# A graph layer on one core: one-hots made slot by slot for both graphs, instead of block by block with a tensor of slot numbers

## The chip, the core and the metric

The kernel runs on one core of a Trainium2 chip. The metric is the device time of the whole program in microseconds (us): 804.08 us, the median of three runs (802.24 to 804.27). The profile is of one execution of 803.91 us, in which the span of the program's instructions is 801.1 us, with a mean granted TensorE clock of 0.995.

Engines are written as in the profile: PE is TensorE's matmuls, PEld its weight loads, DVE is VectorE, ACT ScalarE, POOL GpSimd, SP SyncE, which issues the DMAs. L747 is line 747 of the kernel before.

## The reference

There are 128 graphs of 128 nodes with 64 features each, x [128, 128, 64], and an adjacency matrix for each, adj [128, 128, 128], about 6% of it nonzero, symmetric in its pattern, with the diagonal set. Two layers follow one another, each with a residual and a normalization without gain:

```
mask = adj > 0
h[j,k,:] = relu(x[k] @ W1b-part + x[j] @ W1a/b-part + b1)      # 192 wide, for each pair (j, k)
hm[j] = sum over k of mask[j,k] * h[j,k,:]
x = layernorm(x + hm @ W2 + deg[j] * b2)                        # layer 0
a = adj @ x
o = elu(elu(a @ V1 + c1) @ V2 + c2) @ V3 + c3
x = layernorm(x + o)                                            # layer 1
```

In full, `h[j,k] = relu(x[j] @ W1a + (x[j] - x[k]) @ W1b + b1)`: a part that depends on j alone, called aj, and one that depends on k alone, called cp. The hard part is hm: a sum of relus over the neighbours k of every node j.

## The kernel before, in words

**Only neighbours are visited.** The program takes two graphs (a pair) at a time, 64 pairs in all; the hidden width of 192 is cut into three parts (c) of 64, and the two graphs (s) stand in the two halves of the 128 partitions. For each pair the nodes are sorted by falling degree. `BLOCKS` cuts the 128 sorted positions into nine blocks (p0, p1, s): positions p0 to p1 get s slots each, enough for their neighbours. A block is a unit of work. For a unit with n = s x (p1 - p0) columns:

- ACT fills an `e` bank in PSUM with aj, spread over the slots (L735).
- PE adds, by matmul with a one-hot, the column cp of the neighbour that stands in each slot (`gather`, L742 to L751): three parts k of a bf16 splitting of cp, three parts c, two graphs s, 18 matmuls of n columns. Weights of 64 columns leave half of the array's columns to each graph, so the two streams s = 0 and 1 run side by side.
- DVE takes the absolute sum over the slots (`reduce`, L756). With the sum of absolutes and a correction by degree the relus are had.

There are four `e` banks, `edges`, and unit u uses bank u mod 4; so a unit's fill waits for the reduce of the unit four before. The columns of the nine units are 162, 66, 168, 112, 168, 154, 169, 154 and 170, in this order, 1323 (E) in all.

**The one-hots.** `sort_mask` (L530) sorts the mask, takes prefix sums over the neighbours, and so has in `vp` (128 x 2 x 128, bf16) for each neighbour k (partition), graph and sorted position j the number 2 x slot + 1 if k is j's neighbour in that slot, and an even number if it isn't. A one-hot for slot t is `vp == 2t + 1`. Before, `oh` is [P, 2, E], for each block the slots one after another; nine tensor_tensors (L560) compare vp, spread over the block's slots, with `slotc`, a constant tensor of slot numbers made in the set-up (L159 to L174). Each of them has its own event, and the gather of unit i waits for that of block i. A gather reads `oh[:, s, base:base + n]`, one run without gaps.

**The order of the work.** The program has no loop at run time over the pairs; every instruction is written out, and the order on each engine is set beforehand by a planner, the class `Flow`. Work is cut into threads (Python generators: `prepare`, `sort_x`, `project_a`, `sort_mask`, `turn`, `project_c`, `unit`, `finish`) whose steps name an engine, an estimated cost, what they wait for and how many PSUM banks they want. The planner keeps a clock for each engine and takes next the step that can start first; among steps that can start about as soon on that engine, the one with the earliest due time. A thread's due time advances by `STEP` with each of its steps. `due(p, step)` is `ROUND * (p - AHEAD) + STEP * step`: preparation of pair p is due AHEAD rounds before the pair's gathers. `TURN`, `CS` and `SORT` are the steps at which `turn`, `project_c` and the sort are due. The name PORT beside an engine makes a step of DVE or GpSimd exclude the other's steps of that kind.

PE steps carry a mode: "PE:t" for matmuls with weights of 64 columns (the gathers, L480 and L694), "PE" for the others. A change of mode costs `SWITCH` = 0.1 in the plan, and a step of the other mode ranks as if it were due `HOLD` later. Weights with 64 rows (L593 in `project_c`) are a third shape on the chip, which the planner doesn't tell apart; in the profile the three shapes read 128\*64, 128\*128 and 64\*128.

`finish` (L660) does the rest of layer 0 and layer 1 for a pair. After the last pair, `dense` looks whether any node had more neighbours than its slots and would do such pairs in another way.

Of the kernel before, what the change touches and what calls it, by code (L numbers as in the profile page):

```python
# [31 lines left out]
F32 = mybir.dt.float32  # L32
BF16 = mybir.dt.bfloat16
I32 = mybir.dt.int32
AF = mybir.ActivationFunctionType
OP = mybir.AluOpType
# [6 lines left out]
BLOCKS = ((65, 83, 9), (0, 3, 22), (83, 104, 8), (3, 10, 16), (104, 128, 7), (10, 21, 14),  # L43
          (21, 34, 13), (34, 48, 11), (48, 65, 10))


@with_exitstack
def gnn_kernel(ctx: ExitStack, tc: tile.TileContext, x, adj, w1, b1, w2, b2,
               v1, c1, v2, c2, v3, c3, out):
    nc = tc.nc  # L50
# [4 lines left out]
    P = 128  # L55
# [4 lines left out]
    LAY, E = [], 0  # L60
    for p0, p1, s in BLOCKS:
        n = s * (p1 - p0)
        assert 3 * n <= 512
        LAY.append((E, n, p0, p1, s))
        E += n
    NB = len(LAY)

    cpool = ctx.enter_context(tc.tile_pool(name="consts", bufs=1))
    ctx.enter_context(tc.manual_schedule())
# [4 lines left out]
    def const(shape, dt, name, src=None, pool=cpool):  # L74
        t = pool.tile(shape, dt, name=name)
        if src is not None:
            nc.sync.dma_start(t, src)
        return t

    def temp(shape, dt, name, src=None):  # L80
        return const(shape, dt, name, src, tpool)
# [49 lines left out]
    for s in range(2):  # L131
# [7 lines left out]
                   allow_small_or_imprecise_dtypes=True)  # L139
# [4 lines left out]
                   allow_small_or_imprecise_dtypes=True)  # L144
# [10 lines left out]
                   allow_small_or_imprecise_dtypes=True)  # L155
    nc.vector.tensor_scalar(jcol, jcol, 1.0 / P, None, op0=OP.mult)


    slotf = temp([P, E], F32, "slotf")  # L159
    slots = const([P, 1], F32, "slots")  # L160
    steps = temp([P, 1], F32, "steps")
    nc.vector.memset(slots, 0.0)
    prev = 0
    for base, n, p0, p1, s in LAY:
        nc.gpsimd.iota(slotf[:, base:base + n], pattern=[[2, s], [0, p1 - p0]], base=1,
                       channel_multiplier=0, allow_small_or_imprecise_dtypes=True)
    for p0, p1, s in sorted(BLOCKS, reverse=True):

        nc.vector.tensor_scalar(steps, jcol[:, 0:1], p1 / P, float(s - prev),
                                op0=OP.is_lt, op1=OP.mult)  # L170
        nc.vector.tensor_add(slots, slots, steps)
        prev = s
    slotc = const([P, E], BF16, "slotc")
    nc.vector.tensor_copy(slotc, slotf)  # L174

    srow = const([P, 3, P], F32, "srow")
# [17 lines left out]
    for s in range(2):  # L194
        k = slice(s * F, (s + 1) * F)
# [26 lines left out]
    with tc.tile_pool(name="ps_s", bufs=2, space=bass.MemoryType.PSUM) as ps_s:  # L222
        t = ps_s.tile([P, 512], F32, name="s")
# [4 lines left out]
        t = ps_s.tile([P, 512], F32, name="s")  # L228
# [4 lines left out]
        t = ps_s.tile([P, 512], F32, name="s")  # L233
# [35 lines left out]
class Flow:  # L269
# [10 lines left out]
    NEAR = 0.1  # L280
    NEAR_PE = 0.05
    SWITCH = 0.1
    HOLD = 1

    def __init__(self, banks):
        self.clock = {}
# [45 lines left out]
    def _rank(self, th):  # L332
        engine, _, mode = th[4][0].partition(":")
        return th[0] + (self.HOLD if self._switch(engine, mode) else 0.0), th[1]

# [23 lines left out]
def sparse(tc, env):  # L359

    g = type("env", (), dict(env))
    nc, P, N, F, H, O, HB, H1, NP, E = (
        g.nc, g.P, g.N, g.F, g.H, g.O, g.HB, g.H1, g.NP, g.E)
    LAY, NB = g.LAY, g.NB
    loads, prep, work, ps_m = g.loads, g.prep, g.work, g.ps_m
# [12 lines left out]
    EV = {}  # L378


    ROUND = 11.31
    AHEAD = 3
    PACE = ROUND / NB
    STEP = 1.55
    TURN = 2
    CS = 3
    SORT = 7
    FIN = 1.5

    def due(p, step):  # L390
        return ROUND * (p - AHEAD) + STEP * step

# [30 lines left out]
    def flat(t):  # L423
        return t.rearrange("p s n -> p (s n)")

    def prepare(p):
# [103 lines left out]
    def sort_mask(p, ev):  # L530

        d, a, permb = S[p], ADJ[p], S[p]["permb"]

        def sort(t):
            for s in range(2):
                nc.tensor.matmul(t[:, s * N:(s + 1) * N], d["mk"][:, s, :], permb[:, s, :],
                                 start=True, stop=True)
            for s in range(2):
                nc.tensor.matmul(t[:, (2 + s) * N:(3 + s) * N], permb[:, s, :], identb,
                                 start=True, stop=True)  # L540
        ev, t = yield ("PE", 0.22, [ev], 1, sort)
        mtp = d["mtp"] = prep.tile([P, 2, N], BF16, name="mtp", bufs=7)
        permT = d["permT"] = prep.tile([P, 2, N], F32, name="permT", bufs=7)
        evm, = yield ("ACT", act(2 * N), [ev], 0, lambda: nc.scalar.copy(flat(mtp), t[:, :2 * N]))
        happened(evm, "mtp", p)
        ev, = yield ("ACT", act(2 * N), [ev], 0, lambda: nc.scalar.copy(flat(permT), t[:, 2 * N:]))  # L546
        flow.give(t, ev)
        happened(ev, "permT", p)
        ev, vps = yield ("PE", 0.11, [evm], 1,
                         lambda vps: nc.tensor.matmul(vps[:, :2 * N], g.prefix, flat(mtp),  # L550
                                                      start=True, stop=True))
        vp = prep.tile([P, 2, N], BF16, name="vp")
        ev, = yield ("ACT", act(2 * N), [ev], 0, lambda: nc.scalar.copy(flat(vp), vps[:, :2 * N]))
        flow.give(vps, ev)
        oh = d["oh"] = prep.tile([P, 2, E], BF16, name="oh", bufs=5)
        for i, (base, n, p0, p1, sl) in enumerate(LAY):
            w = p1 - p0
            c = slice(base, base + n)
            ev, = yield ("DVE PORT", 0.08 + n / 960, [ev], 0,
                         lambda: nc.vector.tensor_tensor(  # L560
                             oh[:, :, c].rearrange("p b (s w) -> p b s w", w=w),
                             vp[:, :, p0:p1].rearrange("p b (o w) -> p b o w", o=1)
                             .to_broadcast([P, 2, sl, w]),
                             g.slotc[:, c].rearrange("p (b s w) -> p b s w", b=1, w=w)
                             .to_broadcast([P, 2, sl, w]),
                             op=OP.is_equal))
            happened(ev, "oh", p, i)

    def turn(p):

# [11 lines left out]
        happened(ev, "turned", p)  # L582
        flow.start(due(p, CS), STEP, project_c(p, ev))

# [139 lines left out]

    units = [(p, i) for p in range(NP) for i in range(NB)]

    def unit(u, ev):
        p, i = units[u]
        d = S[p]
        base, n, p0, p1, sl = LAY[i]  # L730
        w = p1 - p0
        e = edges[u % NE][:, :3 * n]
        ev, = yield ("ACT", 0.09 + 3 * n / 1200,
                     [ev, event("aj", p), [T0[0] + pace(u)] if T0 else [0.0]], 0,
                     lambda: nc.scalar.copy(  # L735
                         e.rearrange("p (c s w) -> p c s w", c=3, w=w),
                         d["aj"][:, :, p0:p1].rearrange("p c (o w) -> p c o w", o=1)
                         .to_broadcast([P, 3, sl, w])))
        if not T0:
            T0.append(ev[0])  # L740

        def gather():  # L742
            cp, oh = d["cp"], d["oh"]
            for k in range(3):
                for c in range(3):
                    for s in range(2):
                        nc.tensor.matmul(e[s * HB:(s + 1) * HB, c * n:(c + 1) * n],  # L747
                                         cp[:, k, s, c * HB:(c + 1) * HB],
                                         oh[:, s, base:base + n],
                                         start=False, stop=(k == 2), skip_group_check=True)  # L750
        ev, = yield ("PE:t", 0.03 + 0.0037 * n, [ev, event("cp", p), event("oh", p, i)], 0, gather)  # L751

        def reduce():
            if "sums" not in d:
                d["sums"] = work.tile([P, 3, N], F32, name="sums")
            nc.vector.tensor_reduce(d["sums"][:, :, p0:p1],  # L756
                                    e.rearrange("p (c s w) -> p c w s", c=3, w=w),
                                    AX.X, OP.add, apply_absolute_value=True)
        ev, = yield ("DVE", 0.07 + 3 * n / 960, [ev], 0, reduce)
        happened(ev, "sums", p, i)  # L760
        return ev

# [237 lines left out]
```

## Time and profile before

| what | busy us | share of the span of 801.1 us |
|---|---|---|
| PE | 761.2 | 95% |
| PEld | 687.5 | 86% |
| DVE | 743.1 | 93% |
| ACT | 671.3 | 84% |
| POOL | 431.2 | 54% |

| group | count | busy us | mean ns of one |
|---|---|---|---|
| PE L747, gather | 10368 | 384.5 | 228 |
| DVE L756, reduce over slots | 576 | 338.7 | 606 |
| ACT L735, fill of e | 576 | 312.0 | 553 |
| DVE L560, one-hots | 576 | 172.0 | 335 |

Busy time is the time in which at least one instruction of the group is running. Matmuls are pipelined and their ends are modelled: one of 228 ns doesn't occupy TensorE for 228 ns, and successive ones overlap. So for PE the distances between starts tell more than the durations. The same is true of DVE to a smaller degree.

The first gather starts at 41.5 us and the last at 779.6. Ahead of that are the set-up (constants, 26 us) and the first preparations, behind it the last pairs' `finish`.

### The profile page before, as it was taken

To read this page: it belongs to the slowest core of one execution; us is meant where nothing else is said; L and a number is where in the kernel's file an instruction comes from. 1 tells how busy PE (TensorE), PEld (TensorE's weight loads), DVE (VectorE), ACT (ScalarE), POOL (GpSimd) and SP (SyncE) were. 2 spreads that over 40 slices of the span, in tenths; PEclk is the share of its full clock that TensorE was granted. 3 is DMA by queue.
4 is the path that set the end of the run, shared out by engine and by line. 5 is a ranking of instruction groups with operands and counts; after the bars stand their busy time and mean duration, and the time that the engine had idled before them with its cause. 6 is when DMAs were issued, how large, how long until landed. Compare 5 with 4: busy or idle time off the path is not lost.

```text
span 801.1 us, 35941 instructions
## 1 busy us (share of the span) xinstructions
PE 761.2 (95%) x14550; PEld 687.5 (86%) x14551; DVE 743.1 (93%) x2477; ACT 671.3 (84%) x1858; POOL 431.2 (54%) x787
## 2 busy tenths in 40 slices
PE   2499999999999999999999999999999999999994
PEld 1378889998999999999999999999999999999993
DVE  6689999999999999999999999999999999999983
ACT  0387888988898889889988988898999889988963
POOL 2154465566465556555655665565556556655643
PEclk9999999999999999999999999999999999999997
DMA  1100101111101110110111011101101110111000
GB/s 35 49 3 23 26 19 26 26 22 30 25 20 29 27 28 20 29 27 19 30 30 26 19 30 29 26 20 30 27 21 28 29 26 19 30 29 26 10 10 17
DMA packets 63934, 19.91 MB, mean 25 GB/s; under 512 B 46545, under 2 KB 63762, under 8 KB 63762
## 3 DMA queue, kind: packets, MB, share of 16 engines
q1 hardware_dynamic: 63762, 17.55, 9.6%
q8 instruction: 116, 1.90, 1.0%
q14 instruction: 56, 0.46, 0.2%
HBM read 13.27 MB, written 4.19 MB: 22 GB/s over the span
## 4 chain that ended last, share of the span: by engine, by line
PE 90%; DVE 3%; DMA 2%; SPq 2%; ACT 1%; issue 1%; POOL 0%; ACTq 0%; DVEq 0%; POOLq 0%
PE e L747 43%; PE m L670 6%; PE m L494 6%; PE m L593 5%; PE m L718 4%; PE m L711 3%; PE m L704 3%; PE m L687 3%; PE m L575 2%; PE m L480 2%; PE m L694 2%; PE m L674 1%; PE m L596 1%; DMA adj<-in_adj_dram 1%; PE m L513 1%; PE m L550 1%
## 5 line engine op out<-in xcount | busy, mean ns | idle before, releaser
L747 PE MATMUL e<-oh,cp 128*64 128x162 bf16 (+3 forms) x10368 | 384.5, 228 | 1.5 <-ACT e L735 1.4
L747 PEld LDWEIGHTS <-cp 128*64 128x64 bf16 x10368 | 351.6, 110 | 19.0 <-issue 13.4
L756 DVE TENSOR_REDUCE sums<-e 128x54 f32<-128x486 f32 (+8 forms) x576 | 338.7, 606 | 10.8 <-PE e L747 2.9
L735 ACT COPY e<-aj 128x504 f32<-128x504 f32 (+6 forms) x576 | 312.0, 553 | 41.5 <-DVE sums L756 39.9
L560 DVE TENSOR_TENSOR oh<-vp,slotc 128x336 bf16<-128x336 bf16 (+6 forms) x576 | 172.0, 335 | 0.7 <-PE e L747 0.5
L632 POOL TENSOR_SCALAR ve<-st 128x2 f32<-128x2 f32 x128 | 25.1, 196 | 245.3 <-DVE st L625 238.9
L633 POOL TENSOR_TENSOR rs<-ve,mhalf 128x2 f32<-128x2 f32 x128 | 89.2, 697 | 10.7
L527 POOL TENSOR_TENSOR corr<-ea,sa 128x384 f32<-128x384 f32 x64 | 66.3, 1035 | 38.1 <-DVE ea L520 37.9
L612 POOL TENSOR_TENSOR cp<-r,cp 128x512 bf16<-128x512 f32 x64 | 74.3, 1161 | 10.5 <-ACT cp L610 10.5
L508 POOL TENSOR_TENSOR sa<-aj,srow 128x384 f32<-128x384 f32 x64 | 64.7, 1011 | 15.5 <-ACT aj L501 15.5
L665 POOL TENSOR_TENSOR hm<-sums,corr 128x384 f32<-128x384 f32 x64 | 64.4, 1006 | 9.3 <-DVE sums L756 9.3
L653 ACT ACTIVATE e<-m,mone 128x256 f32<-128x256 f32 x128 | 60.6, 474 | 9.6 <-PE m L704 5.8
L501 ACT ACTIVATE aj<-m,b1c 128x128 f32<-128x128 f32 x192 | 56.7, 368 | 4.9 <-PE m L494 1.7
L656 DVE SCALAR_TENSOR_TENSOR h<-e,m 128x256 f32<-128x256 f32 x128 | 52.9, 413 | 8.5 <-ACT e L653 8.2
L494 PE MATMUL m<-xsT,wad 128*128 128x128 f32 x384 | 59.0, 290 | 0.0
L670 PE MATMUL m<-w2d,hm 128*128 128x128 f32 x384 | 58.4, 288 | 0.7 <-POOL hm L665 0.4
L607 DVE TENSOR_TENSOR r<-m,cp 128x256 f32<-128x256 f32 x128 | 52.6, 413 | 0.1
L643 ACT ACTIVATE x<-y,nb,rs 128x64 f32<-128x64 f32 x128 | 50.7, 458 | 2.1 <-POOL nb L636 2.0
L494 PEld LDWEIGHTS m<-xsT,wad 128*128 128x128 f32 x384 | 48.9, 193 | 3.9 <-ACT permT L546 0.2
L457 DVE SCALAR_TENSOR_TENSOR cmp<-m,keyc,tie 128x128 bf16<-128x128 f32 x128 | 39.7, 347 | 13.3 <-PE m L550 11.1
L670 PEld LDWEIGHTS m<-w2d,hm 128*128 128x128 f32 x384 | 47.9, 192 | 1.8 <-POOL hm L665 0.7
L593 PE MATMUL m<-wc,turned 64*128 64x256 f32 x256 | 45.7, 432 | 0.0
(170 smaller groups left out, 1379.6 us busy)
## 6 DMA issues: line engine op xcount, KB each, us to landing
adj<-in_adj_dram SPq DMA_DIRECT2D x64, 128.0 KB, 2.3
xx<-in_x_dram SPq DMA_DIRECT2D x64, 64.0 KB, 2.2
out_dram<-o SPq DMA_DIRECT2D x64, 64.0 KB, 1.7
degs<-ys SPq DMA_DIRECT2D x64, 1.0 KB, 1.7
w1a<-in_L_gnn_W_dram SPq DMA_DIRECT2D x2, 48.0 KB, 2.1
w1b<-in_L_gnn_W_dram SPq DMA_DIRECT2D x2, 48.0 KB, 2.2
w2s<-in_L_gnn_W_dram SPq DMA_DIRECT2D x2, 48.0 KB, 2.2
b1c<-in_L_gnn_b_dram SPq DMA_DIRECT2D x6, 0.2 KB, 2.3
```

The source lines that it names most:

```text
L494: nc.tensor.matmul(aps[:, c * N:(c + 1) * N], g.wad[:, c, :], xsT, start=True, stop=True)
L508: evs, = yield ("POOL PORT", 0.95, [have], 0, lambda: nc.gpsimd.tensor_mul(sa, aj, g.srow))
L527: ev, = yield ("POOL PORT", 1.05, [ev, evs], 0, lambda: nc.gpsimd.tensor_sub(corr, ea, sa))
L560: lambda: nc.vector.tensor_tensor(oh[:, :, c].rearrange("p b (s w) -> p b s w", w=w), vp[:, :, p0:p1].rearrange("p b (o w) -> p b o w", o= ...
L593: nc.tensor.matmul(cps[s][:, :cols], d["turned"][k, 2, :], g.wc[k, :], start=True, stop=False)
L612: lambda: nc.gpsimd.tensor_sub(cp[:, 2], r1, cp[:, 1]))
L633: nc.gpsimd.tensor_tensor(rs, ve, g.mhalf, op=OP.pow)
L665: lambda: nc.gpsimd.tensor_sub(hm, d["sums"], d["corr"]))
L670: nc.tensor.matmul(yb[:, :2 * O], hm[:, c, :], flat(g.w2d[:, c]), start=(c == 0), stop=False)
L735: lambda: nc.scalar.copy(e.rearrange("p (c s w) -> p c s w", c=3, w=w), d["aj"][:, :, p0:p1].rearrange("p c (o w) -> p c o w", o=1) .to_br ...
L747: nc.tensor.matmul(e[s * HB:(s + 1) * HB, c * n:(c + 1) * n], cp[:, k, s, c * HB:(c + 1) * HB], oh[:, s, base:base + n], start=False, stop ...
L756: nc.vector.tensor_reduce(d["sums"][:, :, p0:p1], e.rearrange("p (c s w) -> p c w s", c=3, w=w), AX.X, OP.add, apply_absolute_value=True)
```

## The change

The one-hots of a pair are made slot by slot instead of block by block. For slot k, one tensor_scalar compares both graphs' `vp[:, :, :w]` with the immediate 2k + 1 and writes two rows of w elements; w is `WIDE[k]`, the last position that has more than k slots, made even. So there are 14 (`ROWS`) such instructions, with w = 128 seven times and then 104, 84, 66, 48, 34, 34, 22. The remaining eight slots, which only positions 0 to 10 have, are made by one tensor_tensor for each graph, with a `slotc` that is now only 8 x 10.

The rows lie in one tile `oh` of [P, EW], EW = 3858 elements: those of the first graph start at 134 k, those of the second at 3730 - 128 k (`RUN`), so that the long rows of the one fill the gaps behind the short rows of the other. A gather of block (p0, p1, s) now reads s rows of p1 - p0 elements at a constant distance of 134 or -128 elements. The purpose is that a comparison with an immediate reads one tensor instead of two.

A gather waits for the whole pair's one-hots (`event("oh", p)`), not its block's. `oh` has four buffers instead of five. The planner's numbers change too: HOLD, ROUND, AHEAD, STEP, TURN, CS, and the estimated cost of the one-hots.

```diff
+ROWS = 14
+RUN = ((0, 134), (3730, -128))
...
+    NS = max(s for p0, p1, s in BLOCKS)
+    WIDE = [max(p1 for p0, p1, s in BLOCKS if s > k) for k in range(NS)]
+    WIDE[ROWS:] = [WIDE[ROWS]] * (NS - ROWS)
+    WIDE = [w + w % 2 for w in WIDE]
...
-    slotf = temp([P, E], F32, "slotf")
+    slotf = temp([P, NS - ROWS, WIDE[ROWS]], F32, "slotf")
...
-    for base, n, p0, p1, s in LAY:
-        nc.gpsimd.iota(slotf[:, base:base + n], pattern=[[2, s], [0, p1 - p0]], base=1,
-                       channel_multiplier=0, allow_small_or_imprecise_dtypes=True)
+    nc.gpsimd.iota(slotf, pattern=[[2, NS - ROWS], [0, WIDE[ROWS]]], base=2 * ROWS + 1,
+                   channel_multiplier=0, allow_small_or_imprecise_dtypes=True)
...
-    HOLD = 1
+    HOLD = 5
...
-    ROUND = 11.31
-    AHEAD = 3
+    ROUND = 11.19
+    AHEAD = 4
     PACE = ROUND / NB
-    STEP = 1.55
-    TURN = 2
-    CS = 3
+    STEP = 1.47
+    TURN = 8
+    CS = 7
...
-        oh = d["oh"] = prep.tile([P, 2, E], BF16, name="oh", bufs=5)
-        for i, (base, n, p0, p1, sl) in enumerate(LAY):
-            w = p1 - p0
-            c = slice(base, base + n)
-            ev, = yield ("DVE PORT", 0.08 + n / 960, [ev], 0,
+        oh = d["oh"] = prep.tile([P, g.EW], BF16, name="oh", bufs=4)
+        WIDE = g.WIDE
+        for k in range(ROWS):
+            w = WIDE[k]
+            at = [b + k * step for b, step in RUN]
+            rows = onehots(oh, at[0], [[at[1] - at[0], 2], [1, w]])
+            last, = yield ("DVE PORT", 0.07 + 2 * w / 3840, [ev], 0,
+                         lambda: nc.vector.tensor_scalar(rows, vp[:, :, :w], 2.0 * k + 1.0, None,
+                                                         op0=OP.is_equal))
+        w, k = WIDE[ROWS], g.NS - ROWS
+        for s, (b, step) in enumerate(RUN):
+            last, = yield ("DVE PORT", 0.08 + k * w / 1920, [ev], 0,
                          lambda: nc.vector.tensor_tensor(
-                             oh[:, :, c].rearrange("p b (s w) -> p b s w", w=w),
-                             vp[:, :, p0:p1].rearrange("p b (o w) -> p b o w", o=1)
-                             .to_broadcast([P, 2, sl, w]),
-                             g.slotc[:, c].rearrange("p (b s w) -> p b s w", b=1, w=w)
-                             .to_broadcast([P, 2, sl, w]),
+                             onehots(oh, b + ROWS * step, [[step, k], [1, w]]),
+                             vp[:, s:s + 1, :w].to_broadcast([P, k, w]), g.slotc,
                              op=OP.is_equal))
-            happened(ev, "oh", p, i)
+        happened(last, "oh", p)
...
-                                         oh[:, s, base:base + n],
+                                         onehots(oh, RUN[s][0] + p0,
+                                                 [[RUN[s][1], sl], [1, w]]),
                                          start=False, stop=(k == 2), skip_group_check=True)
-        ev, = yield ("PE:t", 0.03 + 0.0037 * n, [ev, event("cp", p), event("oh", p, i)], 0, gather)
+        ev, = yield ("PE:t", 0.03 + 0.0037 * n, [ev, event("cp", p), event("oh", p)], 0, gather)
```

More of the change, by code (lines that the diff above doesn't have):

```diff
@@ L66, in gnn_kernel @@
     NB = len(LAY)
+    NS = max(s for p0, p1, s in BLOCKS)
+    WIDE = [max(p1 for p0, p1, s in BLOCKS if s > k) for k in range(NS)]
+    WIDE[ROWS:] = [WIDE[ROWS]] * (NS - ROWS)
+    WIDE = [w + w % 2 for w in WIDE]
+    used = sorted((b + k * step, b + k * step + WIDE[k]) for b, step in RUN for k in range(NS))
+    assert used[0][0] == 0 and all(a[1] <= b[0] for a, b in zip(used, used[1:]))
+    EW = used[-1][1]
     cpool = ctx.enter_context(tc.tile_pool(name="consts", bufs=1))
@@ L172, in gnn_kernel @@
         prev = s
-    slotc = const([P, E], BF16, "slotc")
+    slotc = const([P, NS - ROWS, WIDE[ROWS]], BF16, "slotc")
     nc.vector.tensor_copy(slotc, slotf)
@@ L554, in sort_mask, with onehots @@
         flow.give(vps, ev)
-        oh = d["oh"] = prep.tile([P, 2, E], BF16, name="oh", bufs=5)
-        for i, (base, n, p0, p1, sl) in enumerate(LAY):
-            w = p1 - p0
-            c = slice(base, base + n)
-            ev, = yield ("DVE PORT", 0.08 + n / 960, [ev], 0,
-                         lambda: nc.vector.tensor_tensor(
-                             oh[:, :, c].rearrange("p b (s w) -> p b s w", w=w),
-                             vp[:, :, p0:p1].rearrange("p b (o w) -> p b o w", o=1)
-                             .to_broadcast([P, 2, sl, w]),
-                             g.slotc[:, c].rearrange("p (b s w) -> p b s w", b=1, w=w)
-                             .to_broadcast([P, 2, sl, w]),
+        oh = d["oh"] = prep.tile([P, g.EW], BF16, name="oh", bufs=4)
[10 more added lines that the diff above has]
+            last, = yield ("DVE PORT", 0.08 + k * w / 1920, [ev], 0,
+                         lambda: nc.vector.tensor_tensor(
+                             onehots(oh, b + ROWS * step, [[step, k], [1, w]]),
+                             vp[:, s:s + 1, :w].to_broadcast([P, k, w]), g.slotc,
                              op=OP.is_equal))
-            happened(ev, "oh", p, i)
+        happened(last, "oh", p)
+    def onehots(oh, offset, ap):
+        t = oh[:, offset:offset + 1]
+        return bass.AP(tensor=t.tensor, offset=t.offset, ap=[t.ap[0]] + ap)
     def turn(p):
```

## The prediction

> **What bounds the kernel now.** I read the page first (busy shares, slices, chain), then two windows from the middle of the run, then the order of TensorE's instructions there, then the DVE groups by shape.
>
> From the page, the busy shares and the chain of work that ended last:
>
> ```profile
> PE 761.2 (95%) x14550; PEld 687.5 (86%) x14551; DVE 743.1 (93%) x2477; ACT 671.3 (84%) x1858; POOL 431.2 (54%) x787
> ...
> PE 90%; DVE 3%; DMA 2%; SPq 2%; ACT 1%; issue 1%; POOL 0%; ACTq 0%; DVEq 0%; POOLq 0%
> ```
>
> 90% of the chain is TensorE. Two windows of the steady part (columns: PE, PEld, DVE, ACT, POOL busy, clock, DMA share, GB/s):
>
> ```profile
> 300.00:400.00 100.00, 100.00 (x1964) 91.64 (x1962) 96.66 (x322) 90.35 (x252) 59.14 (x108) 1.00 0.11 26
> 400.00:500.00 100.00, 100.00 (x1974) 91.90 (x1973) 96.95 (x321) 90.35 (x250) 55.71 (x101) 1.00 0.11 26
> ```
>
> PE is at 100%, but DVE is close behind, so neither number says how much slack there is. The order of TensorE's work decides it (start us, us, engine, line):
>
> ```profile
> 401.50 0.61 PE L718 MATMUL m<-v3s,h 128*128 128x64 f32 x4
> 402.03 0.81 PE L747 MATMUL e<-oh,cp 128*64 128x154 bf16 x18
> 402.66 0.41 PE L694 MATMUL m<-turned,x 128*64 128x128 f32 x4
> 402.88 2.12 PE L747 MATMUL e<-oh,cp 128*64 128x169 bf16 x54
> 404.83 0.38 PE L480 MATMUL m<-permf,xx 128*64 128x128 f32 x4
> 405.05 1.09 PE L747 MATMUL e<-oh,cp 128*64 128x162 bf16 x36
> 406.07 0.23 PE L513 MATMUL m<-srow,small 128*128 128x128 bf16 x1
> ...
> 409.22 0.27 PE L550 MATMUL m<-mtp,prefix 128*128 128x256 bf16 x1
> 409.43 1.97 PE L747 MATMUL e<-oh,cp 128*64 128x168 bf16 x54
> 411.32 0.70 PE L593 MATMUL m<-wc,turned 64*128 64x256 f32 x4
> 411.96 0.23 PE L596 MATMUL m<-b2p,onesb 128*128 128x64 bf16 x2
> ```
>
> The same sequence returns every 11.56 us (L593 at 399.76 and at 411.32): one round is one pair of graphs, 64 rounds x 11.56 = 740 of the 801 us. The reader is to see two things. First, a gather unit (18 matmuls of L747, two streams side by side in the two column halves) is packed: at 170 columns successive matmuls of one stream start 73 to 74 ns apart[...], at 66 columns about 28 to 30. Second, each change of array shape costs: from L718 to L747 the starts are 205 ns apart where L718 keeps 109 to 112 within itself, and from L747 (66 columns) to L513 125 ns where 28 is usual. That is 95 ns a change. In this round there are five: into column halves, out, in, to row halves (L593), out. 5 x 0.095 = 0.48 us, so the round is 11.09 us of packed matmuls plus 0.48 of changes. Over 100 to 700 us I count 111 column-half runs, 114 full ones and 51 row-half ones, 276 in 51.9 rounds: 5.3 changes a round.
>
> DVE's one-hots by shape, in the window 300 to 400 us (busy, mean ns, idle before):
>
> ```profile
> L560 DVE TENSOR_TENSOR oh<-vp,slotc 128x336 bf16<-128x336 bf16 x17 | 5.6, 332 | 0.0
> ...
> L560 DVE TENSOR_TENSOR oh<-vp,slotc 128x132 bf16<-128x132 bf16 x8 | 1.9, 238 | 0.0
> ```
>
> 204 elements more cost 94 ns more, 0.46 ns each[...]. What occupies DVE is the distance to the next start: 248 ns at 336, 153 at 132, so 90 ns + 0.47 ns an element. Summing the undisturbed distances (lower tenths) of all DVE work of a round gives 10.6 us, of which the nine one-hots are 2.07. As run they take 2.47, as two blocks are mostly followed by waits. So DVE has under 1 us of slack in 11.56.
>
> [...] No strided moving operand occurs in this trace.
>
> **The change part by part.**
> *One-hots.* Nine tensor_tensors (2.07 us undisturbed) go. Fourteen tensor_scalars come, over 2 x (7x128 + 104 + 84 + 66 + 48 + 34 + 34 + 22) = 2576 elements. [...] Their constant is unknown: [...] above, the 90 ns of today's one-hots; L435's tensor_scalar shows 206 ns for 128 elements[...]. [...] Two tensor_tensors of 80 elements, 0.09 + 0.04 each, add 0.26. [...] DVE gains 0.1 us a round (from -0.1 to +0.3). [...] the planner keeps both apart from its port steps (`PORT`), so I price that at nothing: like for like, in shorter pieces.
> *Gathers.* Same columns, same count. The moving operand becomes rows of 3 to 24 elements instead of one run. Lower bound 0. Upper bound one cycle a row[...]. [...] I take 0[...].
> *The wait.* A gather waits for the whole pair's one-hots instead of its block's. They are planned well over half a round ahead, and behind the waiting matmul stands all of TensorE; but in steady state the pair is ready. At the start the first gather (41.48) comes after its aj (biases at 39.3 to 40.5), the one-hots begin at 38.0 and need 2 us: hidden, at most 1 us.
> *Set-up.* Eight iotas and most of the slot cast (0.84 us) go. The chain to 18 us is SyncE's issues and the last small load, so nothing.
> *Order.* This is where time can come from. HOLD 1 to 5 makes an overdue step of another shape wait for a run to end; AHEAD 3 to 4 and the later TURN and CS put more full-shape work in stock, so it can be taken in one piece. A run of gathers ends when none of the four e banks is refilled. In mid-run the longest has six units (18 + 54 + 36). In the last rounds, where no preparation competes, the runs reach seven (two groups, 36 + 90 matmuls, at 767.51 and 769.01). I take seven as what the new order reaches: 9 / 7 = 1.29 runs a round against 111 / 51.9 = 2.14. That saves 0.85 x 2 x 0.095 = 0.16 us; as L593 then sits less often at a border, I give back 0.02. The round falls to 11.42, and 64 x 0.14 = 9 us: 804 - 9 = 795.
>
> **The rivals.**
> 1. *Nothing moves.* The bank cycle (ACT fill 0.55, gather about 0.6, DVE reduce 0.61 us by their means, with the semaphores between them, over four banks) still ends the runs at six and three units, as DVE gains only 0.1 us. For it: ACT is at 90% and DVE at 97%. Against: the seven-unit runs at the end. Time 803 to 805.
> 2. *Runs of all nine units.* Three changes a round, 11.09 + 0.29 = 11.38, and the looser ramp before 120 us fills better: 64 x 0.19 + 3 = 15, so 789. Against: no run of nine in this trace.
> 3. *Strided reads cost.* With one cycle a row, 26 us come on top: 804 - 9 + 26 = 821[...]. For it: nothing shows such a read at full speed. [...]
> 4. *DVE becomes the bound* (ends slower): [...] sixteen short steps meet GpSimd's 1 us operations more often than nine did. [...] with the reduces late the banks empty: 11.7 a round, 64 x 0.14 = 9 over, 813.
>
> **How the numbers follow.** Forecast 0.50, rival 1 0.15, rival 2 0.12, rival 3 0.12, rival 4 0.11. Faster: 0.50 + 0.12 + a quarter of rival 1, 0.66. Same: half of rival 1 and the edge of rival 3, 0.08. Slower: 0.26. The range goes from 785 (rival 2 with a better ramp) to 814 (rivals 1 and 4, the cheap half of 3); it leaves out the full row penalty and a gain of over 2%. I name the forecast's time, 795.
>
> **What would show it.** Right: fewer column-half runs than 2.14 a round, mostly six or more units in each; L747's starts still 73 ns apart at 170 columns; a round of about 11.4 us; tensor_scalars of 256 elements some 140 ns apart. Wrong: L747 over 75 ns at 170 columns, or worse at 66 columns (22 rows of three), for rival 3; unchanged run counts for rival 1; PE idle gaps that end on DVE's reduces, and tensor_scalars 200 ns or more apart, for rival 4.

## The result, and the profile after

The changed kernel takes 843.16 us (median; 842.45 to 843.27) beside 804.04 us: ratio 1.049, with an interval of 1.0472 to 1.0508. It is 39 us slower. The forecast was 795, the range 785 to 814.

The page after, its busy shares and its chain by engine:

```profile
PE 802.3 (95%) x14550; PEld 727.0 (86%) x14551; DVE 779.5 (93%) x2925; ACT 664.5 (79%) x1858; POOL 431.8 (51%) x779
...
PE 87%; DVE 7%; SPq 2%; ACT 1%; issue 1%; DMA 1%; POOL 1%; ACTq 0%; DVEq 0%; POOLq 0%
```

PE has the same count of matmuls and 41 us more of busy time, and it is still the chain. A window of the steady part:

```profile
400.00:500.00 100.00, 100.00 (x1878) 92.07 (x1874) 97.21 (x361) 83.67 (x237) 55.05 (x100) 1.00 0.10 24
```

PE is full as before, at the full clock, but with 1878 matmuls in this window where there were 1974. A busy share near 100% doesn't prove that TensorE isn't kept waiting (below stands a kernel with 99% in which DVE has half of the chain); the distances between its matmuls, further down, tell more. One round of TensorE:

```profile
404.47 0.28 PE L461 MATMUL m<-identb,degb 128*128 128x128 bf16 x2
...
404.73 1.46 PE L768 MATMUL e<-oh,cp 128*64 128x168 bf16 x36
405.98 0.42 PE L715 MATMUL m<-turned,x 128*64 128x128 f32 x4
406.20 1.55 PE L768 MATMUL e<-oh,cp 128*64 128x168 bf16 x36
...
411.57 0.27 PE L597 MATMUL m<-ident,xx 128*128 128x128 f32 x1
411.78 2.31 PE L768 MATMUL e<-oh,cp 128*64 128x169 bf16 x53
...
415.44 0.70 PE L614 MATMUL m<-wc,turned 64*128 64x256 f32 x4
```

The round is 12.22 us (L614 at 403.22 and 415.44) instead of 11.56. The runs of gathers are of four and five units, not of six and three, and there are still five changes of shape: 251 in 600 us, 5.1 a round, against 5.3. The gathers themselves have grown. By shape, before (L747) and after (L768), busy us and mean ns of one:

```profile
L747 PE MATMUL e<-oh,cp 128*64 128x169 bf16 x1152 | 54.8, 237 | 0.0
L747 PE MATMUL e<-oh,cp 128*64 128x66 bf16 x1152 | 29.3, 195 | 0.0
```

```profile
L768 PE MATMUL e<-oh,cp 128*64 128x169 bf16 x1152 | 64.2, 251 | 0.0
L768 PE MATMUL e<-oh,cp 128*64 128x66 bf16 x1152 | 41.6, 212 | 0.2 <-ACT e L756 0.2
```

The means hide it, since matmuls overlap; the distances between the starts of one stream show it (means between 100 and 700 us; the last column is explained with the rows by themselves):

| block, columns | rows x width | before, ns | after, ns | worked out, ns |
|---|---|---|---|---|
| 66 | 22 x 3 | 32.1 | 47.7 | 49.2 |
| 112 | 16 x 7 | 50.1 | 59.1 | 59.2 |
| 154, two blocks | 14 x 11, 11 x 14 | 69.5 | 74.6 | 75.2 |
| 162 | 9 x 18 | 70.4 | 80.7 | 77.1 |
| 168, two blocks | 8 x 21, 7 x 24 | 74.7 | 79.3 | 80.4 |
| 169 | 13 x 13 | 73.7 | 89.3 | 89.2 |
| 170 | 10 x 17 | 73.9 | 80.1 | 80.4 |

Over the nine blocks the growth is 76.1 ns, over nine steps of each stream 0.685 us a round. The round grew by 0.66. The two agree, so in the steady part the reads account for the whole of it; the experiments ask whether something stands behind them.

### The profile page after: what moved, and what is told of

The parts are those of the page before. It is cut to its first block, busy times and chain, and to the rows that moved or that the text cites. A ratio compares the mean times of both kernels' runs of the same rounds, so it can differ in the third digit from the quotient of the medians.

```text
span 840.6 us, 36518 instructions
## 1 busy us (share of the span) xinstructions
PE 802.3 (95%) x14550; PEld 727.0 (86%) x14551; DVE 779.5 (93%) x2925; ACT 664.5 (79%) x1858; POOL 431.8 (51%) x779
## 4 chain that ended last, share of the span: by engine, by line
PE 87%; DVE 7%; SPq 2%; ACT 1%; issue 1%; DMA 1%; POOL 1%; ACTq 0%; DVEq 0%; POOLq 0%
PE e L768 43%; PE m L507 6%; PE m L691 5%; PE m L614 4%; PE m L732 3%; PE m L739 3%; PE m L725 3%; PE m L708 3%; DVE sums L778 2%; DVE oh L575 2%; PE m L493 2%; PE m L715 2%; PE m L596 2%; PE m L695 1%; PE m L617 1%
## 5 line engine op out<-in xcount | busy, mean ns | idle before, releaser
L768 PE MATMUL e<-oh,cp 128*64 128x162 bf16 (+3 forms) x10368 | 429.9, 236 | 0.3 <-ACT e L756 0.2
L768 PEld LDWEIGHTS <-cp 128*64 128x64 bf16 x10368 | 399.3, 109 | 18.3 <-issue 10.6
L756 ACT COPY e<-aj 128x504 f32<-128x504 f32 (+6 forms) x576 | 306.6, 542 | 85.3 <-DVE sums L778 82.4
L778 DVE TENSOR_REDUCE sums<-e 128x54 f32<-128x486 f32 (+8 forms) x576 | 331.2, 607 | 8.2 <-PE e L768 5.8
L575 DVE TENSOR_SCALAR oh<-vp 128x256 bf16<-128x256 bf16 (+6 forms) x896 | 196.3, 267 | 0.5
L654 POOL TENSOR_TENSOR rs<-ve,mhalf 128x2 f32<-128x2 f32 x128 | 89.2, 697 | 10.6
L540 POOL TENSOR_TENSOR corr<-ea,sa 128x384 f32<-128x384 f32 x64 | 64.3, 1005 | 38.5 <-DVE oh L575 34.8
L686 POOL TENSOR_TENSOR hm<-sums,corr 128x384 f32<-128x384 f32 x64 | 64.1, 1001 | 25.8 <-DVE sums L778 23.1
L691 PE MATMUL m<-w2d,hm 128*128 128x128 f32 x384 | 56.7, 284 | 0.5 <-DVE permb L478 0.3
L601 ACT COPY turned<-m 128x384 f32<-128x384 f32 x64 | 31.3, 490 | 31.8 <-PE m L597 31.8
L533 DVE SCALAR_TENSOR_TENSOR ea<-aj,m 128x384 f32<-128x384 f32 x64 | 35.3, 552 | 18.0 <-PE m L528 15.0
L653 POOL TENSOR_SCALAR ve<-st 128x2 f32<-128x2 f32 x128 | 24.8, 194 | 49.4 <-DVE st L646 42.4
```

The costliest lines, as they stand in the source:

```text
L540: ev, = yield ("POOL PORT", 1.05, [ev, evs], 0, lambda: nc.gpsimd.tensor_sub(corr, ea, sa))
L575: lambda: nc.vector.tensor_scalar(rows, vp[:, :, :w], 2.0 * k + 1.0, None, op0=OP.is_equal))
L654: nc.gpsimd.tensor_tensor(rs, ve, g.mhalf, op=OP.pow)
L691: nc.tensor.matmul(yb[:, :2 * O], hm[:, c, :], flat(g.w2d[:, c]), start=(c == 0), stop=False)
L756: lambda: nc.scalar.copy(e.rearrange("p (c s w) -> p c s w", c=3, w=w), d["aj"][:, :, p0:p1].rearrange("p c (o w) -> p c o w", o=1) .to_br ...
L778: nc.vector.tensor_reduce(d["sums"][:, :, p0:p1], e.rearrange("p (c s w) -> p c w s", c=3, w=w), AX.X, OP.add, apply_absolute_value=True)
```

## The experiments

The label in brackets is the name by which the expectations speak of a kernel. Theory: the strided moving operand of the gathers, that is the one-hots read in rows, costs 0.66 us a round. Rivals: the new order, or DVE, whose short tensor_scalars wait for GpSimd.

**Reads of one run (e1).** The changed kernel, but a gather takes n elements in a row, so it multiplies by other values of the same buffer, and its result isn't the layer's:

```diff
-                                         onehots(oh, RUN[s][0] + p0,
-                                                 [[RUN[s][1], sl], [1, w]]),
+                                         oh[:, 2976 + 432 * s:2976 + 432 * s + n],
```

> The changed kernel, but each gather reads n elements in one run (from the first graph's long rows' part of the tile, which has no gaps) instead of its rows; it thereby takes the wrong one-hots, everything else is the same. Theory: the whole loss is the strided moving operand; in the changed kernel two-step distances between gather matmuls grew by 5 to 16 ns a block, 0.685 us a round summed over nine passes. Then these fall back to those of before (74 ns at 170 columns, 30 to 32 at 66), the round to 11.5 to 11.6 us, the time to 798 to 806 us. Rival: the loss is in the order or in DVE (tensor_scalars that wait for GpSimd): then the time stays above 830 us.

Measured: 816.9 us, ratio 1.0194 (1.0177 to 1.0211). Both theories missed. The distances fell back, 73.4 ns at 170 columns and 32.2 at 66, so the reads are real: 3.0 points of the 4.9% went with them, some 24 us. But 1.9%, 15 us, stayed. The round is 11.87 us in the mean, and the page's chain has turned over:

```profile
DVE 49%; PE 33%; ACT 7%; issue 6%; SPq 2%; DMA 1%; POOL 1%; ACTq 0%; DVEq 0%; POOLq 0%
```

Without the reads' cost DVE has the largest share of the chain, though PE is busy for 98.8% of the time between 300 and 400 us and for 99.4% between 400 and 500. What DVE loses stands in one window of the changed kernel (DVE and GpSimd, start us, us):

```profile
410.45 0.55 DVE L533 SCALAR_TENSOR_TENSOR ea<-aj,m 128x384 f32<-128x384 f32 x1 [0.36 <-PE m L528]
410.93 1.58 DVE L575 TENSOR_SCALAR oh<-vp 128x256 bf16<-128x256 bf16 x5
411.15 1.00 POOL L540 TENSOR_TENSOR corr<-ea,sa 128x384 f32<-128x384 f32 x1 [0.54 <-DVE oh L575]
```

Five tensor_scalars (of 256, 168, 256, 132 and 256 elements; the line names the first) take 1.58 us instead of some 0.75: undisturbed ones start 114 ns (132 elements) to 142 ns (256) apart. GpSimd's correction needs `ea`, which ends at 411.01, and starts at 411.15, between two of the tensor_scalars. The one that DVE begins next, at 411.18, lasts 1.06 us, until 0.08 us after the correction's end. The correction doesn't wait for a one-hot: `ea` and the one-hots raise the same semaphore, so the view names the last of them. It starts 145 ns after the end of `ea` here and 144 ns after it in the kernel before (medians), where the page names `ea` itself and a single one-hot stands beside it, the next one 1.7 us later:

```profile
L527 POOL TENSOR_TENSOR corr<-ea,sa 128x384 f32<-128x384 f32 x64 | 66.3, 1035 | 38.1 <-DVE ea L520 37.9
```

```profile
406.55 0.55 DVE L520 SCALAR_TENSOR_TENSOR ea<-aj,m 128x384 f32<-128x384 f32 x1
407.02 0.42 DVE L560 TENSOR_TENSOR oh<-vp,slotc 128x224 bf16<-128x224 bf16 x1
...
408.70 0.33 DVE L560 TENSOR_TENSOR oh<-vp,slotc 128x336 bf16<-128x336 bf16 x1
```

Between 200 and 600 us of the changed kernel the one-hots last 30.3 us longer than undisturbed ones, 22.7 of it beside this correction (L540) and 7.1 beside L686; before, they lost 4.7.

**The order alone (e2).** The kernel before with the changed planner numbers:

```diff
-    HOLD = 1
+    HOLD = 5
...
-    ROUND = 11.31
-    AHEAD = 3
+    ROUND = 11.19
+    AHEAD = 4
-    STEP = 1.55
-    TURN = 2
-    CS = 3
+    STEP = 1.47
+    TURN = 8
+    CS = 7
```

> The kernel before with the changed kernel's planner numbers alone (HOLD, ROUND, AHEAD, STEP, TURN, CS). The theory that only reads cost says 798 to 806 us: changes of array shape went only from 5.3 to 5.1 a round, worth 0.02 us a round, 1 to 2 us. The rival that the new order itself is worse says over 815 us. My prediction's hope of seven-unit runs would say 793 to 797.

Measured: 820.9 us, ratio 1.0236 (1.0219 to 1.0253), and 362 changes of shape in 600 us, 7.2 a round of 11.9 us instead of 5.3. The new numbers are bad for the old one-hots. The rival's statement held (over 815 us), the other two missed. It doesn't carry over to the changed kernel, where the same numbers give 5.1 changes a round. The nine long one-hots lose 5.4 us in the same 400 us here, so it isn't the planner numbers alone that bring the 30.3.

**The changed one-hots in the old order (e3)** (the same edit backwards, in the changed kernel):

> The changed kernel with the planner numbers of before. The theory that reads cost says 838 to 850 us, with the same distances within the gathers as in the changed kernel. The rival that the order is to blame says 800 to 812 us.

Measured: 927.05 us, ratio 1.157 (1.1537 to 1.1594), with the gathers' distances of the changed kernel. The reading part held; the time missed by 77 us. PE has 55% of the chain, DVE 22%, ACT 15%, in rounds of 13.7 us, and the one-hots lose 26.7 us in 400. A gather waits for all sixteen one-hots, and sixteen steps of STEP 1.55 with AHEAD 3 fall due late by the plan's own sum (16 x 1.55 = 24.8 of 33.9 us, after the steps ahead of them); that this is the cause is not shown. So the new numbers and the new one-hots belong together, and the effect of either alone can't be read from a sum.

**The reads by themselves (e4).** A kernel that computes no layer, only pairs of bf16 matmuls with 64 weight columns, 40 pairs of each form, in one execution:

> The disputed cost by itself: no layer is computed, only pairs of bf16 matmuls (64 weight columns, two streams in the two column halves, 40 of each form, about 168 columns), whose moving operand is one run or rows of 24, 13, 8, 7, 6, 4, 3, 2 or 1 elements from different first elements; some forms with one stream, with both streams on the same rows, or with one stream in a run. Runs should stay at 72 to 73 ns from an even or an odd first element. Theory of lines: a row costs by the 16-byte lines it touches, so rows of 8 from element 0 cost nothing, from element 4 or 1 more, rows of 2 and 1 far more. Theory of rows: every row adds the same, whatever its first element, so 8 from 0 and 8 from 4 are alike, and 21 rows of 8 add three times what 7 rows of 24 add. [...]

Measured, the distance between the starts in one stream (two streams at once unless said otherwise; the first element is counted from a multiple of eight bf16 elements, 16 bytes, in the tile; such a stretch of eight is called a line here, and the timings below bear it out):

| moving operand, 168 or 169 columns | ns |
|---|---|
| one run, from element 0 / 1 | 72.5 / 73.3 |
| 7 rows of 24, from 0 / 4 | 72.5 / 73.4 |
| 21 rows of 8, from 0 | 72.4 |
| 21 rows of 8, from 4 / 2 / 1 | 73.4 / 86.5 / 93.5 |
| 24 rows of 7, from 0 / 5 | 82.5 / 86.7 |
| 28 rows of 6, 42 rows of 4, from 0 | 72.5, 72.9 |
| 13 rows of 13, from 0 (at full clock) / 7 / 5 | 79 / 89.4 / 88.8 |
| 56 rows of 3, 84 rows of 2, 168 rows of 1, from 0 | 113.2, 148.7, 304 |
| one stream alone: run, 21 of 8, 56 of 3, 84 of 2 | 72.5, 72.5, 113.3, 148 |
| both streams on the same rows: 21 of 8, 56 of 3 | 72.5, 113.3 |

A row as such costs nothing: 42 rows of 4 run like one run (72.9 and 72.5 ns). Nor is it a matter of single elements: rows of 2 have none and take twice the time (148.7 ns). Nor do the two streams get in each other's way: one alone costs the same (148 ns with rows of 2). What fits best is this, an estimate from these timings: each piece of a row that lies inside one 16-byte line takes at least the time of four elements. 84 pieces of 2 are then 84 x 4 / 2.4 + 2.5 = 142.5 ns (148.7 measured). The 2.4 columns a nanosecond are the slope between runs of 66 and of 170 columns, 30 and 73 ns (medians of the kernel with reads of one run); the 2.5 is what one run of 168 takes over 168 / 2.4. A row of 13 from element 7 is cut into 1, 8 and 4 elements, priced 4 + 8 + 4 = 16, and 13 x 16 / 2.4 + 2.5 = 89.2 ns (89.4 measured); from element 5 it is cut into 3, 8 and 2, the same 89.2 (88.8). Rows of 8 from element 2 are 6 + 2, priced 10, so 90.0 ns (86.5), and from element 1 they are 7 + 1, 98.8 (93.5). The length of eight comes from these rows too: cut at every sixteenth element, those from element 2 would stay whole, 72.5 ns, and at every fourth they would be 2 + 4 + 2, priced 12, 107.5 ns, where 86.5 were measured. The rule is too low for odd widths: rows of 3 (95.8 by the rule, 113.2 measured), rows of 7 from element 0 (72.5 and 82.5), rows of 13 from element 0 (72.9 and 79). Odd widths have something of their own, which I did not take apart.

With the rule, the offsets of all rows in both batches, and the slower batch of each block, one gets the last column of the table in the result. For the nine blocks it gives 6.00 us a round, where the measured distances sum to 5.98. The growth is 0.83 by the rule and 0.685 measured, since the kernel before took 5.30 us where the same formula gives 5.16 for runs.

**Where the rows lie (e5, e6).** If the price hangs on the line pieces, then moving the rows against the lines changes the time, with the count of rows, the widths, and the rest of the work left alone. Two kernels, in each of which the placement alone is changed: rows that cross lines more often, and rows that cross them less.

```diff
-RUN = ((0, 134), (3730, -128))
+RUN = ((4, 136), (3766, -128))
```

> The changed kernel with the rows placed otherwise: 4 + 136 k and 3766 - 128 k, same number and width of rows, same DVE work, same order. Theory of line pieces (each piece of a row inside one 16-byte line takes at least four elements' time, from the run of rows by themselves): summed over the nine blocks with the slower graph in each, the gathers take 6.32 us a round instead of 5.79, so the round grows from 12.22 by about 0.5 us and the time to 865 to 885 us; the block of 66 columns and those of 168 to 170 are spread further. Theory of rows (a fixed price a row): 841 to 846 us, as the changed kernel.

```diff
-RUN = ((0, 134), (3730, -128))
+RUN = ((0, 136), (3762, -128))
```

> The same with the best placement of rows found by that sum: 136 k and 3762 - 128 k, 5.68 us a round instead of 5.79. Theory of line pieces: 0.11 us a round less, 834 to 840 us. Theory of rows: 841 to 846 us.

Measured: 873.12 us for the first, ratio 1.0891 (1.0866 to 1.0917), with a round of 12.76 us: 0.54 over the changed kernel, where the rule gave 0.525 (the distances alone give 0.41). The second took 838.71 us, 1.0456 (1.0434 to 1.0477), in rounds of 12.15: 0.07 less, where the rule gave 0.11. Both times lie in the ranges that the pieces gave. A steady window of the first, and its chain:

```profile
400.00:500.00 100.00, 100.00 (x1794) 91.43 (x1789) 92.71 (x348) 79.84 (x227) 52.92 (x96) 1.00 0.10 24
```

```profile
PE 92%; DVE 3%; SPq 2%; ACT 1%; DMA 1%; issue 1%; POOL 0%; ACTq 0%; DVEq 0%; POOLq 0%
```

PE is still full, with 1794 matmuls in this window, 84 fewer than in the changed kernel, and 180 fewer than before. The width of the rows can't tell the three placements apart, nor can a price per row; the pieces can. Nor is it the distance from row to row: the two new placements have the same (136 and -128) and differ only in the first element, by four. The shortest block shows it best: 66 columns take 73.8 ns in the first (75.8 by the rule), 47.7 in the changed kernel (49.2), 43.4 in the second (39.2). Single blocks are off by up to 9 ns: 169 columns in the first are 72.9 by the rule and 81.9 measured.

**GpSimd's hold on DVE (e7).** In the kernel with reads of one run, 15 us over the kernel before were left. If they come from tensor_scalars that are held while GpSimd's correction runs, a shorter correction must take them away. This kernel is the one with reads of one run, and it computes the correction for one of its three parts only, which stands for the other two:

```diff
-        corr = d["corr"] = prep.tile([P, 3, N], F32, name="corr", bufs=7)
-        ev, = yield ("POOL PORT", 1.05, [ev, evs], 0, lambda: nc.gpsimd.tensor_sub(corr, ea, sa))
+        corr = d["corr"] = prep.tile([P, 1, N], F32, name="corr", bufs=7)
+        ev, = yield ("POOL PORT", 1.05, [ev, evs], 0, lambda: nc.gpsimd.tensor_sub(corr, ea[:, 0:1], sa[:, 0:1]))
...
-                     lambda: nc.gpsimd.tensor_sub(hm, d["sums"], d["corr"]))
+                     lambda: nc.gpsimd.tensor_sub(hm, d["sums"],
+                                                      d["corr"].to_broadcast([P, 3, N])))
```

> The kernel of e1 (the changed one with gathers that read runs, thus the wrong one-hots) in which GpSimd's correction is computed for one part of three and used for all (so it leaves out two thirds of it); the planned costs and so the order are unchanged. In e1 DVE has 49% of the chain, its round is 11.85 us, and tensor_scalars of the one-hots lose 32 us in 400 while one GpSimd instruction runs, 22.7 of it beside this correction of 1.0 us. Theory of the port: with the correction at about 0.35 us DVE gains some 0.4 us a round, PE becomes the bound again at 11.5 to 11.6 and the time falls to 797 to 803 us. Rival (DVE is bound by its sixteen instructions or by the order itself): the time stays at 813 to 818 us.

Measured: 798.05 us, ratio 0.9949 (0.9932 to 0.9966), in rounds of 11.48 us. The theory held; "port" in it is the kernel's mark `PORT`, and what in the chip makes the one-hot last no run here shows. The groups by shape between 300 and 500 us, first with the whole correction, then with the short one (busy us, mean ns, idle before and what ended it):

```profile
L575 DVE TENSOR_SCALAR oh<-vp 128x256 bf16<-128x256 bf16 x118 | 39.6, 335 | 0.1
...
L540 POOL TENSOR_TENSOR corr<-ea,sa 128x384 f32<-128x384 f32 x17 | 17.0, 1001 | 6.9 <-DVE oh L575 6.2 <-DVE ea L533 0.7
```

```profile
L575 DVE TENSOR_SCALAR oh<-vp 128x256 bf16<-128x256 bf16 x123 | 33.2, 270 | 0.1
...
L540 POOL TENSOR_TENSOR corr<-ea,sa 128x128 f32<-128x128 f32 x17 | 7.7, 456 | 8.3 <-DVE oh L575 7.6 <-DVE ea L533 0.7
```

The correction still starts 145 ns after `ea`, but takes 0.46 us instead of 1.00: the one-hot that it holds lasts 0.51 us instead of 1.06, the mean tensor_scalar falls from 335 to 270 ns, and the one-hots' loss in 400 us from 32.0 to 17.9 us. GpSimd itself has 1% of the chain or less in both kernels, so it is through DVE that the shorter correction acts. With that DVE drops behind PE again, and the chain returns to TensorE:

```profile
PE 85%; DVE 9%; SPq 2%; ACT 1%; issue 1%; DMA 1%; POOL 0%; ACTq 0%; DVEq 0%; POOLq 0%
```

It is the only kernel here below 804 us, but it reads the wrong one-hots and leaves two thirds of a step out, so it is no version to keep. Since it runs in the changed kernel's order (5.1 changes of shape a round, runs of four and five units), that order isn't what made the change slow.

**Do the two costs add? (e10)** The short correction alone, in the changed kernel with its rows as they are (again one part of three is computed):

> The changed kernel, rows and all, with the correction computed for one part of three as in e7 (two thirds of it left out). With runs instead of rows this shortening took 817 to 798 us. Theory: with rows PE has no gap left in its 12.22 us round, so the port's waits lie under it and the time stays at 836 to 843 us; the reads then cost about 42 us where DVE is free, and the two losses do not add. Rival (they add): 822 to 827 us.

Measured: 841.41 us, ratio 1.0494 (1.0476 to 1.0512): nothing gained that can be told from noise. A steady window:

```profile
400.00:500.00 100.00, 100.00 (x1872) 91.76 (x1866) 93.72 (x359) 85.36 (x240) 51.43 (x102) 1.00 0.11 25
```

DVE's busy share fell from 97.2% to 93.7% in this window, and PE still has no gap and does no more matmuls (1872 and 1878). The four corners:

| us (ratio to before) | whole correction | one part of three |
|---|---|---|
| gathers of one run | 816.9 (1.0194) | 798.05 (0.9949) |
| gathers by rows | 843.16 (1.049) | 841.41 (1.0494) |

The runs of one column and of the other were beside the kernel before at 802 to 804 us, so I take the ratios, in hundredths of 804 us. Rows cost 5.45 (44 us) where DVE is out of the way and 2.96 (24 us) where it isn't; the whole correction costs 2.45 (20 us) where the reads are cheap and nothing that can be told where they aren't. Together they make 4.9 - (-0.51) = 5.41 (43 us), not 5.45 + 2.45 = 7.9: in the changed kernel DVE's waits lie under TensorE's longer gathers.

**The late start (e8).** The first gather begins at 50.5 us instead of 41.5, since it now waits for all sixteen one-hots of its pair, and these come between other pairs' steps on DVE. To see what that costs, the first pair's one-hots fall due 60 us earlier:

```diff
-        flow.start(due(p, SORT), STEP, sort_mask(p, ev))
+        flow.start(due(p, SORT) - (60 if p == 0 else 0), STEP, sort_mask(p, ev))
```

> The changed kernel, with the first pair's one-hots due 60 us earlier in the plan, so that its sixteen steps are not mixed with the other pairs' preparation. Theory that the whole-pair wait costs 7 us at the start (first gather at 50.5 us instead of 41.5): the first gather comes at 42 to 45 us and the time falls by 4 to 8 us, 834 to 839. Rival (the early rounds win the late start back): 841 to 845.

Measured: 842.3 us, ratio 1.05 (1.048 to 1.052). The first gather comes at 45.0 us, 5.5 earlier, and the end doesn't move: from the first gather to the last it takes 774.9 us instead of 768.8. By the fifth pair the two kernels stand at 92.7 and 93.1 us. The rival held.

**The order in the kernel before (e11, e9).** Two small edits there, to see whether the count of changes of shape can be brought down at all. First HOLD alone:

```diff
-    HOLD = 1
+    HOLD = 5
```

> The kernel before with HOLD 5 in place of 1 and nothing else, for the step of my prediction that let longer runs of gathers follow from it. That step says fewer than 5.3 changes of shape a round and 793 to 800 us. The rival, after the kernel of e2 had 7.2 changes a round, says that HOLD does not lengthen the runs: 800 us or more, and no fewer changes.

Measured: 813.72 us, ratio 1.0146 (1.0129 to 1.0163), 297 changes in 600 us, 5.8 a round instead of 5.3, and the rival held. Runs of seven units do occur (18 in these 600 us, none before), but beside more short ones: the mean run falls from 4.2 units to 3.8. Second, the projection (L593 before) given its own kind, so that the planner sees that it changes the shape:

```diff
-        ev, *cps = yield ("PE", 0.7, [ev], 2, project)
+        ev, *cps = yield ("PE:r", 0.7, [ev], 2, project)
```

> The kernel before, with project_c (weights of 64 rows) given a mode of its own in the plan, so that the planner sees all changes of the array's shape. If the 95 ns a change are what can still be had in the order, and the planner finds an order with one change less a round, the time falls by up to 6 us, to 796 to 800. If the order only moves, 800 to 806.

Measured: 815.45 us, ratio 1.0174 (1.016 to 1.0188), 317 changes, 6.2 a round. Both expectations missed. Either edit moves the whole order that the planner finds, and the time with it by 1 to 2%. So a difference of this size between two orders is not the effect of the one rule that was changed.

## Why the prediction was wrong

The prediction put 9 us of gain on the order and nothing on the reads; the runs showed next to no gain from the order (5.1 changes of shape a round against 5.3) and a loss of 0.66 us a round from the reads, 42 us in 64 rounds. By its steps:

- **The reads: the step that failed.** "I take 0" was the author's estimate, and nothing in the trace before could show it, as each of its gathers reads one run. The gathers grew by 0.685 us a round, the round by 0.66. Pair by pair, the changed kernel's gathers start 2.2 us behind those of before at the third pair and 41.2 at the 62nd, 0.66 us a round, and the last gather comes 39.8 later, as the last rounds give 1.4 back; that is the 39. Not even the upper bound held, one column's time for each row (at the 2.4 columns a nanosecond of the runs, 110 rows x 9 / 2.4 = 0.41 us a round), and the runs with moved rows show that the same number of rows costs 0.59 to 1.20 us a round, depending on where they lie (12.15 and 12.76 less the old 11.56). Rival 3 named this outcome and its sign, and gave 821 at most; the range should have had a wider bound on that side.
- **The order.** "I take seven as what the new order reaches." It reached runs of four and five units, and 5.1 changes a round against 5.3, worth 0.02 us. HOLD alone makes 5.8. At the end of the kernel before, where runs of seven stood, no preparation work competes; I took it for the middle, where it does. What else ends the runs in the middle no run here shows.
- **DVE's time.** Right in its outcome, though how fast a tensor_scalar would run was the author's estimate, which no trace showed then: undisturbed tensor_scalars of 256 elements start 142 ns apart (the prediction said some 140), those of 132 elements 114, so an element takes 0.23 ns by this slope, where it takes 0.47 in the tensor_tensors before (248 ns at 336 elements, 153 at 132). The undisturbed one-hots of a round sum to 1.8 to 2.0 us, beside 2.07 before, and the step that DVE gains about 0.1 us holds for the work, not for the waits.
- **The contention.** "I price that at nothing" failed: DVE's one-hots lose 30.3 us in 400, 0.9 a round, nearly all of it beside GpSimd's two long operations, where nine longer tensor_tensors lost 4.7 us in 400. In the kernel before, five one-hots lasted over 1 us, 1.18 at most, beside a median of 0.33. What I missed is that GpSimd gets in between two one-hots that follow one another, and that the one begun next then lasts as long as GpSimd's instruction (1.06 us beside a correction of 1.00), however short it is by itself. Why the two meet so much more often now is not settled: the loss goes with the new one-hots (30.3 and 26.7 us with either set of planner numbers, 4.7 and 5.4 with the old one-hots), but the planner also places them elsewhere. The loss happens to be hidden in the changed kernel, by the other failure; without the rows it would have cost 15 us (816.9), near to rival 4's 813, which was an estimate.
- **The wait for the whole pair.** "Hidden, at most 1 us": the first gather is 9 us later, so the size was wrong. The end doesn't feel it, as the run with the earlier one-hots shows.
- **The bound.** Right: TensorE has 90% of the chain before and 87% after, at full clock, and in the changed kernel relief for DVE alone gave nothing (841.41 us).

Of the rivals, the third came true: its term, 0.41 us a round at most, measured 0.66, and the 9 us of gain that it was set against were not there.

## What to carry to other kernels

As the runs here estimate it: before an operand of TensorE is laid out in short rows, cut each row at the 16-byte lines and count every piece as at least four bf16 elements; where all pieces have four, six or eight elements, the rows here ran like one run (73.4 ns at most, beside 72.5), while rows of 3, of 7 and of 13 took up to 18% more than this count. Where many short instructions of DVE may meet a long one of GpSimd, price each meeting by GpSimd's duration, not by DVE's (1.06 us beside 1.00 here, 0.51 beside 0.46), and look in the trace how often they meet. And a cost that lies under the bound today turns up when the bound is taken away: the two here were worth 24 to 44 and 0 to 20 us, depending on the other.

## What the runs showed of the hardware

- A bf16 moving operand is read at full rate from rows of 4 elements at a distance of 128 bytes (72.9 ns for 168 columns, 72.5 as one run), and at half rate from rows of 2 (148.7 ns).
- GpSimd doesn't wait for a pause of DVE: its correction starts 145 ns after its input is there, between back-to-back tensor_scalars, and the tensor_scalar begun just after lasts until 0.08 us after its end, 1.06 us beside a correction of 1.00 us (384 f32 elements), 0.51 beside one of 0.46 (128).
- Two streams in the two column halves go in step: where one reads one run and the other rows of 2, the steady part takes 149 ns for each pair of matmuls, as if both had rows of 2, though the run alone needs 72.5. Only at the beginning does the run's stream get ahead by a few.
- In the kernel of the reads by themselves the clock record falls to half between 70.7 and 77.5 us (8, 5 and 7 tenths in the slices below). It begins in the midst of back-to-back matmuls whose rows hold one element each (63.0 to 74.9 us), and these stay 304 ns apart through the fall, so their price doesn't follow the granted clock. The next form, rows of 13 from element 0, takes 141 ns until 77.5 us and 79 after it. The slices of the page, the nineteenth to the twenty-first place:

```profile
PE   0999999999999999999999999999996000000000
...
PEclk9999999999999999998579999999999655555555
```

PE is busy throughout, and the clock comes back 2.4 us after the next form began. This is one execution, and no run here tells whether the slow reads are the cause of the fall.

Left open are the price of odd widths (rows of 3, 7 and 13), how often GpSimd meets the one-hots and why, and what makes the planner find a good order. No version here beats the kernel before at its full work.
